# A two-layer graph network: layer 2's counts transposed by VectorE, the order of the passage between the layers given, and buffers of x split by use

## The chip, the cores and the metric

The kernel runs on one core of a Trainium2 chip. Times are microseconds of device time for one execution of the whole kernel. Engines are named as in the profile: PE (TensorE), PEld (its weight loads), DVE (VectorE), ACT (ScalarE), POOL (GpSimd, which issues the gathers), SP (which issues all other transfers).

## The reference

There are N = 2500 nodes of D = 1024 features and E = 80,000 edges, with `dst` sorted and skewed towards low nodes. Cut to what matters:

```python
# layer 1
support = relu(layernorm(x)) @ W0
x = x + segment_sum(support[src] * edge_weight[:, None], dst)
# layer 2: edge_index = [src, dst], with self loops
h = relu(layernorm(x)) @ W1.T + b
deg = counts of row (self loops included)
norm = deg[row] ** -0.5 * deg[col] ** -0.5
x = x + segment_sum(norm[:, None] * h[col], row)
```

`row` and `col` of layer 2 are src and dst with the self loops added. Layer 2 is thus out = x1 + S A S h, where A holds how often each pair of nodes is joined (plus the identity) and S is the diagonal of deg to the power -1/2.

## The kernel before

Rows are cut into NT = 20 tiles of P = 128 (the last has 68), features into KC = 8 slices of 128 or two halves of H = 512.

**Support.** For each row tile, layernorm, relu and 16 matmuls (L293) give the rows of `support`, which go to DRAM. This ends at about 470 us. Beside it, and in the stage that follows, VectorE and PE build the tables of counts: one-hot rows (L458, L460), a matmul (L462), and an addition into `counts` (L472), a 128 x 20 x 128 table for each destination tile, in three buffers that are taken in turn. `cleared` (L429) sets a table to zero on ACT (L435) before its first use. A finished table is stored to DRAM as `cnat` (L523) in 256-byte pieces.

**Gather stage.** The first DENSE = 4 tiles have so many edges that they are multiplied as dense tables against all of `support` (L657), two tiles and one half of the columns at a time. The 16 others ("thin" tiles) are handled in 378 blocks of 128 edges: POOL gathers 128 rows of `support` into `msg` (L616, eight buffers), ACT scales them and rounds to `hi` (L622), DVE computes the remainder `lo` (L624), and four matmuls with a one-hot matrix sum them by row (L628). When a thin tile is summed, `finish` (L568) adds x to the sums (L581; x is loaded at L163 by `load_rows`), stores x1 (L583) and normalizes; its rows are transposed on PE (L562, copied by ACT at L563), multiplied by W1 (L597, `second_rows`), get the bias on DVE (L601), and are stored as `hid_d` (L604). Dense tiles store their halves of x1 (L668) and come back through L573. Before the change both kinds of `xt`, the thin tiles' and the dense tiles', are buffers of one ring of two in the pool `work`.

How these streams are interleaved is decided by a planner in the kernel's own Python (`takes`, `count`, `others`), which keeps an estimate of the time of PE, DVE and ACT. On each engine instructions run in their order of issue. `order_behind` adds an ordering between two instructions of one engine and no wait between engines.

**Passage.** After the last gather the loop over layer 2 begins while the last tile's transposes and products are still running. `split(k)` (L810) loads hidden tile k (L812, three buffers, on SP), scales it by `dis` on ACT (hi, L813) and forms the remainder on DVE (lo, L814). `dis` holds deg to the power -1/2 with row t x 128 + p in partition p, column t (L787 to L790). `counts_of(r)` (L819) loads the counts of row tile r transposed, by one DMA transpose (L822), and ACT casts them to f32r in two halves of ten k (L828; four buffers `bT`).

**Rows.** `multiply` (L854) accumulates hi and lo of all 20 k in PSUM (L858, 80 matmuls a row tile), and `row` (L831) adds x1 and stores `out` (L836, L838). Row tiles 0 and 1 run as a pair, k by k behind `split`; 2 to 19 follow alone. The last tile runs its two column halves one after the other in one PSUM tile and adds both after the end.

Of the kernel before, what the change touches and what calls it, by code (L numbers as in the profile page):

```python
# [42 lines left out]
KEPT = 3  # L43

EARLY = 9

ORDER = (3, 4, 5, 6, 2, 7, 8, 9, 1, 10, 11, 12, 13, 0, 14, 15, 16, 17, 18, 19)

# [2 lines left out]
def direct(  # L51
# [41 lines left out]
    def rows(t):  # L93
        return min(P, N - t * P)
# [1 line left out]
    keep = ctx.enter_context(tc.tile_pool(name="keep", bufs=1))  # L96
    dram = ctx.enter_context(tc.tile_pool(name="dram", bufs=1, space=bass.MemoryType.DRAM))
    support = dram.tile([N, D], F32, name="support")
    cnat = dram.tile([NT, NT, P, P], F16, name="cnat")
    x1_d = [dram.tile([P, D], F32, name=f"x1_d{t}") for t in range(NT)]  # L100
    hid_d = [dram.tile([P, D], F32, name=f"hid_d{t}") for t in range(NT)]

    ident = keep.tile([P, P], F32, name="ident")
    make_identity(nc, ident)
# [51 lines left out]
        nc.scalar.activation(hn, xt, AF.Relu, scale=rstd[:, 0:1], bias=mean[:, 1:2])  # L156
        return hn

    def load_rows(t, pool):
        xt = pool.tile([P, D], F32, name="xt")  # L160
        if rows(t) < P:
            nc.vector.memset(xt, 0.0)
        nc.sync.dma_start(xt[:rows(t), :], x[t * P:t * P + rows(t), :])  # L163
        return xt
# [257 lines left out]
    KW = NT * max(w for _, w in WINDOWS)  # L422
    bases = {}
    ahead = None
    to_store = []
    dense = {}
    counts = {}

    def cleared(t):  # L429


        if t in counts:
            return
        counts[t] = cpool.tile([P, NT, P], F16, name="counts", bufs=3)
        i = nc.scalar.copy(counts[t].rearrange("p t w -> p (t w)"), zero.to_broadcast([P, NT * P]))  # L435
        if len(counts) > 3:
            order_behind(i, last_count)
# [117 lines left out]
    gpool = first.enter_context(tc.tile_pool(name="gather", bufs=2, side="right", reuse_waits="tile"))  # L555


    def transposed(v, into):
        for k0 in range(0, KC, 4):
            pT = psum.tile([P, 4, P], F32, name="pT")  # L560
            for k in range(4):
                nc.tensor.transpose(pT[:, k, :], v[:, (k0 + k) * P:(k0 + k + 1) * P], ident)  # L562
            nc.scalar.copy(into[:, k0:k0 + 4, :], pT)  # L563
            yield 0.7, 0.0, 0.6

    PIECES = 8
# [1 line left out]
    def finish(t, sums=None):  # L568


        if sums is None:
            xt = work.tile([P, D], F32, name="xt")
            nc.sync.dma_start(xt, x1_d[t])  # L573
            sum_ = work.tile([P, 1], F32, name="sum_")
            nc.vector.tensor_add(sum_, halves[t][:, 0:1], halves[t][:, 1:2])
            for _ in range(3):
                yield 0.0, 0.0, 0.0
        else:
            xt = load_rows(t, work)
            sum_ = work.tile([P, 1], F32, name="sum_")  # L580
            nc.vector.scalar_tensor_tensor(xt, sums.rearrange("p h d -> p (h d)"), 1.0, xt,  # L581
                                           op0=ALU.mult, op1=ALU.add, accum_out=sum_)
            nc.sync.dma_start(x1_d[t], xt)  # L583
# [7 lines left out]
    def second_rows(t, vT):  # L591

        hid = work.tile([P, D], F32, name="hn")
        for h in range(2):
            mm = psum.tile([P, 4, P], F32, name="pT").rearrange("p a b -> p (a b)")
            for k in range(KC):
                on_pe(nc.tensor.matmul(mm, vT[:, k, :], w1_sb[k][:, h * H:(h + 1) * H],  # L597
                                       start=(k == 0), stop=(k == KC - 1)))
                if k % 2 and k < KC - 1:
                    yield 1.75, 0.0, 0.0  # L600
            nc.vector.tensor_add(hid[:, h * H:(h + 1) * H], mm, bias[:, h * H:(h + 1) * H])  # L601
            if h == 0:
                yield 1.75, 0.65, 0.0
        nc.sync.dma_start(hid_d[t], hid)  # L604
        yield 1.75, 0.65, 0.0

    drawn = []
    last_hi = None

    def gathered(t, sums):  # L610
        nonlocal last_hi
        n = TILE_BLOCKS[t]
        for j in range(n):
            k = K0[t] + j
# [5 lines left out]
            nc.vector.tensor_scalar(oh, iota, row_p[:, k:k + 1], None, op0=ALU.is_equal)  # L620
            hi = gpool.tile([P, D], F32R, name="hi")
            last_hi = nc.scalar.activation(hi, msg, AF.Copy, scale=wgt_p[:, k:k + 1])  # L622
            lo = gpool.tile([P, D], F32R, name="lo")
            nc.vector.scalar_tensor_tensor(lo, msg, wgt_p[:, k:k + 1], hi.bitcast(F32),  # L624
                                           op0=ALU.mult, op1=ALU.subtract)
            for v in (hi, lo):
                for h in range(2):
                    i = nc.tensor.matmul(  # L628
# [9 lines left out]
    def multiplied(ts):  # L638
# [5 lines left out]
        for h in range(2):  # L644
            sums = psum_m.tile([P, 2, H], F32, name="mm")
            cols = slice(h * H, (h + 1) * H)
            for k0 in range(0, NT, 2):
# [7 lines left out]
                for k in (k0, k0 + 1):  # L655
# [151 lines left out]
    for k in range(EARLY):  # L807
        parts_of(k, early)

    def split(k):  # L810
        hf = work.tile([P, D], F32, name="rows", bufs=3)
        order_behind(nc.sync.dma_start(hf, hid_d[k]), drawn[-1])  # L812
        order_behind(nc.scalar.activation(his[k], hf, AF.Copy, scale=dis[:, k:k + 1]), last_hi)  # L813
        nc.vector.scalar_tensor_tensor(los[k], hf, dis[:, k:k + 1], his[k].bitcast(F32),  # L814
                                       op0=ALU.mult, op1=ALU.subtract)

    HALF = NT // 2

    def counts_of(r):  # L819

        cT = work.tile([P, NT, P], F16, name="cT")
        i = nc.sync.dma_start_transpose(out=cT.rearrange("p t s -> p (t s)"),  # L822
                                        in_=cnat[r].rearrange("t p d -> (t p) d"))
        order_behind(i, drawn[-1])
        bTs = []
        for k in (0, HALF):
            bTs.append(work.tile([P, HALF, P], F32R, name="bT", bufs=4))
            order_behind(nc.scalar.copy(bTs[-1], cT[:, k:k + HALF, :]), last_hi)  # L828
        return bTs

    def row(r, mm, hs):  # L831
        xh = work.tile([P, D], F32, name="rows", bufs=3)
        nc.sync.dma_start(xh, x1_d[r])
        for h in hs:
            cols = slice(h[0] * H, (h[-1] + 1) * H)
            nc.vector.scalar_tensor_tensor(xh[:, cols], mm.rearrange("p h d -> p (h d)")[:, cols],  # L836
                                           dis[:, r:r + 1], xh[:, cols], op0=ALU.mult, op1=ALU.add)
            nc.sync.dma_start(out[r * P:r * P + rows(r), cols], xh[:rows(r), cols])  # L838

    def all_placed():  # L840

# [12 lines left out]
    def multiply(bTs, mms, k, hs):  # L854
        for v in (his[k], los[k]):
            for bT, mm in zip(bTs, mms):
                for h in hs:
                    nc.tensor.matmul(mm[:, h, :], bT[k // HALF][:rows(k), k % HALF, :],  # L858
                                     v[:rows(k), h * H:(h + 1) * H],
                                     start=(k == 0 and v is his[k]), stop=(k == NT - 1 and v is los[k]))  # L860


    for rs in [(0, 1)] + [(r,) for r in range(2, NT)]:
        bTs = [counts_of(r) for r in rs]
        mms = [psum.tile([P, 2, H], F32, name="mm2", bufs=3) for r in rs]
        hs = ((0,), (1,)) if rs == (NT - 1,) else ((0, 1),)
        for part in hs:
            for k in range(NT):
                if rs[0] == 0:
                    split(k)  # L870
                multiply(bTs, mms, k, part)
        for r, mm in zip(rs, mms):
            row(r, mm, hs)
        if rs[0] == 4:
            all_placed()


def kernel(tc, edges, xT, *args):
# [338 lines left out]
```

## Time and profile before

| What | us |
|---|---|
| median of 3 runs (1697.03 to 1700.88) | 1699.94 |
| profiled execution, its own time | 1699.42 |
| span of its trace | 1697.6 |
| mean granted PE clock | 0.989 |

The span is what the trace covers; the execution's own time has some 1.8 us around it. Part of the groups of the profile, with their busy time and the mean of one instruction, then the idle time just ahead of them on their engine and who ended most of it:

```profile
L622 ACT ACTIVATE hi<-msg,wgt_p 128x1024 fp32r<-128x1024 f32 x378 | 425.6, 1146 | 279.1 <-PE mm L628 218.0
L624 DVE SCALAR_TENSOR_TENSOR lo<-msg,wgt_p,hi 128x1024 fp32r<-128x1024 f32 x378 | 478.1, 1280 | 31.9 <-ACT hi L622 23.6
L597 PE MATMUL pT<-w,vT 128*128 128x512 f32 x640 | 305.4, 595 | 0.0
L828 ACT CAST bT<-cT 128x1280 fp32r<-128x1280 f16 x40 | 50.2, 1263 | 262.9 <-PE mm L858 255.7
```

In a line such as the second, `lo<-msg,wgt_p,hi` names the tile written and the tiles read, `128x1024` partitions by elements, and `x378` the number of instructions. Matmuls overlap, so their mean is longer than the distance between two of them (0.226 us in the rows, 0.43 for L597). In a timeline a line starts with its start time and its length in us, and the bracket at its end tells how long its engine had been idle and what released it.

### The profile page before, as it was taken

How to read it: one execution, taken by the hardware profiler on the slowest of the kernel's cores; microseconds unless marked ns; L12 is line 12 of the kernel's file. 1: busy time of each engine (PE TensorE's matmuls, PEld its weight loads, DVE VectorE, ACT ScalarE, POOL GpSimd, SP SyncE). 2: the span in 40 equal slices, each digit the busy share in tenths (PEclk: the TensorE clock that was granted, in tenths of full speed). 3: DMA queues.
4: the chain of work that ended last, by engine and by line, in shares of the span. 5: the costliest groups of instructions: out<-in, count | busy, mean ns of one | idle time of the engine just before them, and what ended most of it. 6: DMA issues, size and time to landing. Idle time of an engine off the chain costs nothing.

```text
span 1697.6 us, 21231 instructions
## 1 busy us (share of the span) xinstructions
PE 1637.2 (96%) x6506; PEld 1033.2 (61%) x6506; DVE 1182.1 (70%) x3044; ACT 926.3 (55%) x1536; POOL 528.0 (31%) x501
## 2 busy tenths in 40 slices
PE   6999999999979998999999999999998999999998
PEld 2465555554435555565656666666654788888886
DVE  5778888889869997999999999998886410000000
ACT  3299999991125655666656666666666311111110
POOL 3000000000037665656656666666660000000000
PEclk9999999999989999999999999999999999999999
DMA  7512221123289998889899998999899634333320
GB/s 256 190 63 66 79 66 54 52 71 87 70 299 322 362 306 308 310 305 317 289 336 350 321 329 313 355 319 327 300 304 251 214 109 109 93 81 108 93 65 33
DMA packets 213657, 351.57 MB, mean 207 GB/s; under 512 B 115358, under 2 KB 134824, under 8 KB 213534
## 3 DMA queue, kind: packets, MB, share of 16 engines
q0 software_dynamic: 60592, 219.74, 36.9%
q1 hardware_dynamic: 152942, 130.39, 25.0%
q8 instruction: 53, 0.87, 0.2%
q14 instruction: 70, 0.57, 0.1%
HBM read 282.41 MB, written 54.56 MB: 198 GB/s over the span
## 4 chain that ended last, share of the span: by engine, by line
PE 63%; DMA 3%; issue 2%; DVE 2%; ACT 1%; POOL 1%; SPq 1%; DVEq 0%; POOLq 0%; ACTq 0%
PE mm L858 21%; PE mm L628 18%; PE pT L597 15%; PE mm L657 5%; PE cb L462 2%; DMA msg<-support,src_p 2%; PE pT L562 1%; DVE lo L624 1%; DMA rows<-hid_d 1%; PE mm L293 1%; DMA xt<-in_x 1%; SPq L822 0%; POOL msg L616 0%; DMA x_d<-xt 0%; ACT hi L622 0%
## 5 line engine op out<-in xcount | busy, mean ns | idle before, releaser
L622 ACT ACTIVATE hi<-msg,wgt_p 128x1024 fp32r<-128x1024 f32 x378 | 425.6, 1146 | 279.1 <-PE mm L628 218.0
L616 POOL DMA_INDIRECT msg<-support,src_p x378 | 480.4, 1271 | 273.1 <-DVE lo L624 117.9
L624 DVE SCALAR_TENSOR_TENSOR lo<-msg,wgt_p,hi 128x1024 fp32r<-128x1024 f32 x378 | 478.1, 1280 | 31.9 <-ACT hi L622 23.6
L293 PE MATMUL mm<-w,hT 128*128 128x512 f32 x640 | 317.0, 608 | 2.4 <-ACT hT L185 2.4
L597 PE MATMUL pT<-w,vT 128*128 128x512 f32 x640 | 305.4, 595 | 0.0
L628 PE MATMUL mm<-hi,oh_r 128*128 128x512 f32 x756 | 294.4, 470 | 5.0 <-DVE xt L581 5.0
L628 PE MATMUL mm<-lo,oh_r 128*128 128x512 f32 x756 | 264.1, 430 | 3.0 <-DVE lo L624 2.7
L469 ACT ACTIVATE wl<-oh_low,wpart 128x128 bf16<-128x128 bf16 x891 | 261.8, 394 | 0.0
L858 PE MATMUL mm<-lo,bT 128*128 128x512 f32 (+1 forms) x800 | 247.1, 390 | 0.0
L858 PE MATMUL mm<-hi,bT 128*128 128x512 f32 (+1 forms) x800 | 247.0, 390 | 0.0
L836 DVE SCALAR_TENSOR_TENSOR rows<-mm,dis,rows 128x1024 f32<-128x1024 f32 (+1 forms) x21 | 25.7, 1233 | 311.6 <-PE mm L858 311.6
L460 DVE TENSOR_SCALAR oh_key<-iota,key 128x200 bf16<-128x200 f16 (+12 forms) x675 | 195.6, 292 | 4.4 <-PE cb L476 4.3
L828 ACT CAST bT<-cT 128x1280 fp32r<-128x1280 f16 x40 | 50.2, 1263 | 262.9 <-PE mm L858 255.7
L628 PEld LDWEIGHTS mm<-hi,oh_r 128*128 128x128 f32 x756 | 140.5, 190 | 81.1 <-issue 45.4
L628 PEld LDWEIGHTS mm<-lo,oh_r 128*128 128x128 f32 x756 | 138.9, 189 | 70.1 <-DVE lo L624 22.0
L597 PEld LDWEIGHTS pT<-w,vT 128*128 128x128 f32 x640 | 120.9, 190 | 83.6 <-issue 68.7
L858 PEld LDWEIGHTS mm<-lo,bT 128*128 128x128 f32 (+1 forms) x800 | 150.2, 188 | 32.0 <-issue 0.5
L458 DVE TENSOR_SCALAR oh_low<-iota,low 128x128 bf16<-128x128 f16 x675 | 167.5, 252 | 2.3 <-ACT wl L469 1.7
L858 PEld LDWEIGHTS mm<-hi,bT 128*128 128x128 f32 (+1 forms) x800 | 150.1, 188 | 31.3
L472 DVE TENSOR_TENSOR counts<-cb,counts 128x200 f32 (+13 forms) x296 | 138.8, 469 | 43.1 <-PE cb L462 35.7
L657 PE MATMUL mm<-msg,dense 128*128 128x512 f32 (+1 forms) x320 | 153.8, 598 | 0.0
L293 PEld LDWEIGHTS mm<-w,hT 128*128 128x128 f32 x640 | 109.2, 195 | 65.8 <-issue 60.1
(172 smaller groups left out, 1179.4 us busy)
## 6 DMA issues: line engine op xcount, KB each, us to landing
msg<-support POOLq DMA_DIRECT2D x36, 512.0 KB
xt<-in_x SPq DMA_DIRECT2D x34, 512.0 KB
cnat<-counts SPq DMA_DIRECT2D x20, 640.0 KB
hid_d<-hn SPq DMA_DIRECT2D x20, 512.0 KB
rows<-hid_d SPq DMA_DIRECT2D x20, 512.0 KB
rows<-x_d SPq DMA_DIRECT2D x20, 512.0 KB
hT<-in_xT SPq DMA_DIRECT2D x19, 512.0 KB
support<-row SPq DMA_DIRECT2D x19, 512.0 KB
```

Of the source, the lines that this page charges most:

```text
L293: on_pe(nc.tensor.matmul(mm[:, h, :], vT[:, k, :], ws[k][:, h * H:(h + 1) * H], start=(k == 0), stop=(k == KC - 1)))
L458: nc.vector.tensor_scalar(oh_low, iota16[:, :P], low[:, k:k + 1], None, op0=ALU.is_equal)
L460: nc.vector.tensor_scalar(oh_key[:, :NT * w], iota16[:, :NT * w], key[:, k:k + 1], None, op0=ALU.is_equal)
L469: nc.scalar.activation(wl[:, i, :], oh_low, AF.Copy, scale=wpart[:, i, k:k + 1])
L472: nc.vector.tensor_tensor(to, cb[:, :NT * w].rearrange("p (t w) -> p t w", w=w), to, op=ALU.add)
L597: on_pe(nc.tensor.matmul(mm, vT[:, k, :], w1_sb[k][:, h * H:(h + 1) * H], start=(k == 0), stop=(k == KC - 1)))
L616: drawn.append(nc.gpsimd.indirect_dma_start(out=msg, out_offset=None, in_=support, in_offset=bass.IndirectOffsetOnAxis(ap=src_p[:, k:k + 1 ...
L622: last_hi = nc.scalar.activation(hi, msg, AF.Copy, scale=wgt_p[:, k:k + 1])
L624: nc.vector.scalar_tensor_tensor(lo, msg, wgt_p[:, k:k + 1], hi.bitcast(F32), op0=ALU.mult, op1=ALU.subtract)
L628: i = nc.tensor.matmul(sums[:, h, :], oh, v[:, h * H:(h + 1) * H], start=(j == 0 and v is hi), stop=(j == n - 1 and v is lo))
L657: m = nc.tensor.matmul(sums[:, i, :], dense[t][:rows(k), k, :], msg[:rows(k), k - k0], start=(k == 0), stop=(k == NT - 1))
L858: nc.tensor.matmul(mm[:, h, :], bT[k // HALF][:rows(k), k % HALF, :], v[:rows(k), h * H:(h + 1) * H], start=(k == 0 and v is his[k]), stop ...
```

## The change

It has five parts.

1. **Counts of layer 2.** `cnat` is laid out as [tile, row, tile, column], so that one row's counts are contiguous. A row tile's counts are loaded as they lie by four transfers in runs of 1280 bytes (`cN`, one buffer), transposed on DVE in blocks of 32 x 32 (one StreamTranspose of 128 x 2560 f16 a row tile, `cT`, one buffer), and cast by ACT with a reordering of 32-element runs. The blocks stay in their group of 32 partitions, so step k of the product takes hidden rows 32k to 32k + 31 of each of four quarters of 640 rows. The hidden rows are stored in five DRAM tiles in which those rows can be loaded by one transfer; steps 18 and 19 have 100 and 96 rows. `dis` is stored to DRAM and loaded again in the new order of rows (`dis_k`).
2. **Order of the passage.** Loads of hidden rows for k of 3 and more are ordered behind the loads of row 1's counts and behind the last x1 store; their hi behind ACT's last copy of the second transposes; their lo behind the last bias addition. The StreamTransposes stand behind the last lo of the gather stage. Row 2's counts are loaded behind the hidden rows of k = 10.
3. **First rows' scaling.** The first four hi of the gather stage are ordered behind the latest clearing of a counts table.
4. **x buffers by use.** Thin tiles have one buffer `xt`, dense tiles one buffer `dense_xt`, in place of the shared ring of two.
5. **Last row tile.** x1 is loaded ahead, the two column halves have PSUM tiles of their own, and each half is added and stored after its own matmuls.

On PE only the first pair of rows changes: between the two groups of four transposes only hi of row 0 for k = 0 stays, and the rest of that step follows the 32 products of L597. On SP, 80 loads of counts and 5 transfers of dis take the place of 20 DMA transposes. POOL's order is unchanged.

The diff, cut to its core:

```diff
-    cnat = dram.tile([NT, NT, P, P], F16, name="cnat")
+    cnat = dram.tile([NT, P, NT, P], F16, name="cnat")
+    dis_d = dram.tile([NT, P], F32, name="dis_d")
-    hid_d = [dram.tile([P, D], F32, name=f"hid_d{t}") for t in range(NT)]
+    hid_d = [dram.tile([4, P, D], F32, name=f"hid_d{q}") for q in range(NT // 4)]
...
-        i = nc.scalar.copy(counts[t].rearrange("p t w -> p (t w)"), zero.to_broadcast([P, NT * P]))
+        last_clear = nc.scalar.copy(counts[t].rearrange("p t w -> p (t w)"), zero.to_broadcast([P, NT * P]))
...
-            i = nc.sync.dma_start(cnat[:, t].rearrange("k p d -> p k d"), counts[t])
+            i = nc.sync.dma_start(cnat[:, :, t, :].rearrange("k p d -> p k d"), counts[t])
...
-            xt = work.tile([P, D], F32, name="xt")
+            xt = work.tile([P, D], F32, name="dense_xt", bufs=1)
...
-            xt = load_rows(t, work)
+            xt = load_rows(t, work, bufs=1)
...
             last_hi = nc.scalar.activation(hi, msg, AF.Copy, scale=wgt_p[:, k:k + 1])
+            if len(drawn) <= 4:
+                order_behind(last_hi, last_clear)
...
-                        xt = work.tile([P, 2, H], F32, name="xt")
+                        xt = work.tile([P, 2, H], F32, name="dense_xt", bufs=1)
...
+    nc.sync.dma_start(dis_d.rearrange("t p -> p t"), dis)
+    dis_k = keep.tile([P, NT], F32, name="dis_k")
+    for u in range(4):
+        nc.sync.dma_start(dis_k[32 * u:32 * u + 32, :],
+                          dis_d.rearrange("t p -> (t p)")[u * NT * 32:(u + 1) * NT * 32]
+                          .rearrange("(k i) -> i k", i=32))
...
     def split(k):
         hf = work.tile([P, D], F32, name="rows", bufs=3)
-        order_behind(nc.sync.dma_start(hf, hid_d[k]), drawn[-1])
...
+        of = hid_d[32 * k // P][:, 32 * k % P:32 * k % P + 32, :]
...
+        for j in i:
+            order_behind(j, drawn[-1] if k < AT_ONCE else loaded_counts[1])
+            if k >= AT_ONCE:
+                order_behind(j, last_x1)
...
+        order_behind(hi, last_hi if k < AT_ONCE else last_copy)
...
+        if k >= AT_ONCE:
+            order_behind(lo, last_bias)
...
-        cT = work.tile([P, NT, P], F16, name="cT")
-        i = nc.sync.dma_start_transpose(out=cT.rearrange("p t s -> p (t s)"),
-                                        in_=cnat[r].rearrange("t p d -> (t p) d"))
-        order_behind(i, drawn[-1])
+        cN = work.tile([P, 4, QUARTER], F16, name="cN", bufs=1)
+        for u in range(4):
+            i = nc.sync.dma_start(
+                cN[32 * u:32 * u + 32],
+                cnat[r].rearrange("(q i) t d -> i q (t d)", q=4)[:, :, u * QUARTER:(u + 1) * QUARTER])
+            order_behind(i, loads[HALF] if r == 2 else drawn[-1])
+        loaded_counts.append(i)
+        cT = work.tile([P, 4, NT, 32], F16, name="cT", bufs=1)
+        i = nc.vector.transpose(cT.rearrange("p q k i -> p (q k i)"), cN.rearrange("p q x -> p (q x)"))
+        order_behind(i, last_lo)
...
-            order_behind(nc.scalar.copy(bTs[-1], cT[:, k:k + HALF, :]), last_hi)
+            order_behind(nc.scalar.copy(bTs[-1].rearrange("p k q i -> p q k i"), cT[:, :, k:k + HALF, :]), last_hi)
...
-    for rs in [(0, 1)] + [(r,) for r in range(2, NT)]:
+    for rs in [(0, 1)] + [(r,) for r in range(2, NT - 1)]:
...
+    bTs = [counts_of(NT - 1)]
+    xh = x1_of(NT - 1)
+    for h in range(2):
+        mm = psum.tile([P, 2, H], F32, name="mm2", bufs=3)
+        for k in range(NT):
+            multiply(bTs, [mm], k, (h,))
+        row_of(NT - 1, xh, slice(h * H, (h + 1) * H), mm[:, h, :])
```

AT_ONCE is 3, QUARTER is 640 and HALF is 10.

More of the change, by code (lines that the diff above doesn't have):

```diff
@@ L45 @@
 EARLY = 9
+AT_ONCE = 3
 ORDER = (3, 4, 5, 6, 2, 7, 8, 9, 1, 10, 11, 12, 13, 0, 14, 15, 16, 17, 18, 19)
@@ L157, in normed, with load_rows @@
         return hn
-    def load_rows(t, pool):
-        xt = pool.tile([P, D], F32, name="xt")
+    def load_rows(t, pool, **bufs):
+        xt = pool.tile([P, D], F32, name="xt", **bufs)
         if rows(t) < P:
@@ L424, in direct @@
     ahead = None
+    last_clear = None
     to_store = []
@@ L434, in cleared @@
         counts[t] = cpool.tile([P, NT, P], F16, name="counts", bufs=3)
-        i = nc.scalar.copy(counts[t].rearrange("p t w -> p (t w)"), zero.to_broadcast([P, NT * P]))
+        nonlocal last_clear
+        last_clear = nc.scalar.copy(counts[t].rearrange("p t w -> p (t w)"), zero.to_broadcast([P, NT * P]))
         if len(counts) > 3:
-            order_behind(i, last_count)
+            order_behind(last_clear, last_count)
         if t < DENSE:
@@ L555, in direct @@
     gpool = first.enter_context(tc.tile_pool(name="gather", bufs=2, side="right", reuse_waits="tile"))
+    last_copy = last_bias = last_x1 = None
     def transposed(v, into):
+        nonlocal last_copy
         for k0 in range(0, KC, 4):
@@ L562, in transposed @@
                 nc.tensor.transpose(pT[:, k, :], v[:, (k0 + k) * P:(k0 + k + 1) * P], ident)
-            nc.scalar.copy(into[:, k0:k0 + 4, :], pT)
+            last_copy = nc.scalar.copy(into[:, k0:k0 + 4, :], pT)
             yield 0.7, 0.0, 0.6
@@ L582, in finish @@
                                            op0=ALU.mult, op1=ALU.add, accum_out=sum_)
-            nc.sync.dma_start(x1_d[t], xt)
+            nonlocal last_x1
+            last_x1 = nc.sync.dma_start(x1_d[t], xt)
             yield 0.0, 1.25, 0.0
@@ L591, in second_rows @@
     def second_rows(t, vT):
+        nonlocal last_bias
         hid = work.tile([P, D], F32, name="hn")
@@ L600, in second_rows @@
                     yield 1.75, 0.0, 0.0
-            nc.vector.tensor_add(hid[:, h * H:(h + 1) * H], mm, bias[:, h * H:(h + 1) * H])
+            last_bias = nc.vector.tensor_add(hid[:, h * H:(h + 1) * H], mm, bias[:, h * H:(h + 1) * H])
             if h == 0:
                 yield 1.75, 0.65, 0.0
-        nc.sync.dma_start(hid_d[t], hid)
+        nc.sync.dma_start(hid_d[t % (NT // 4)][t // (NT // 4)], hid)
         yield 1.75, 0.65, 0.0
     drawn = []
-    last_hi = None
+    last_hi = last_lo = None
     def gathered(t, sums):
-        nonlocal last_hi
+        nonlocal last_hi, last_lo
         n = TILE_BLOCKS[t]
@@ L622, in gathered @@
             last_hi = nc.scalar.activation(hi, msg, AF.Copy, scale=wgt_p[:, k:k + 1])
+            if len(drawn) <= 4:
+                order_behind(last_hi, last_clear)
             lo = gpool.tile([P, D], F32R, name="lo")
-            nc.vector.scalar_tensor_tensor(lo, msg, wgt_p[:, k:k + 1], hi.bitcast(F32),
-                                           op0=ALU.mult, op1=ALU.subtract)
+            last_lo = nc.vector.scalar_tensor_tensor(lo, msg, wgt_p[:, k:k + 1], hi.bitcast(F32),
+                                                     op0=ALU.mult, op1=ALU.subtract)
             for v in (hi, lo):
@@ L808, in direct, with valid @@
         parts_of(k, early)
+    QUARTER = NT * P // 4
+    HALF = NT // 2
+    loads, loaded_counts = [], []
+    def valid(k):
+        return min(P, 96 + max(N - 3 * QUARTER - 32 * k, 0))
     def split(k):
         hf = work.tile([P, D], F32, name="rows", bufs=3)
[L812 to L815, printed above, removed]
@@ L817, in direct @@
-    HALF = NT // 2
-    def counts_of(r):
-        cT = work.tile([P, NT, P], F16, name="cT")
-        i = nc.sync.dma_start_transpose(out=cT.rearrange("p t s -> p (t s)"),
-                                        in_=cnat[r].rearrange("t p d -> (t p) d"))
-        order_behind(i, drawn[-1])
+        of = hid_d[32 * k // P][:, 32 * k % P:32 * k % P + 32, :]
+        m = valid(k)
+        if m == P:
+            i = [nc.sync.dma_start(hf, of)]
+        else:
+            i = [nc.sync.dma_start(hf[:96], of[:3])]
+            if m > 96:
+                i.append(nc.sync.dma_start(hf[96:m], of[3, :m - 96, :]))
@@ new lines, in split @@
+        for j in i:
+            order_behind(j, drawn[-1] if k < AT_ONCE else loaded_counts[1])
+            if k >= AT_ONCE:
+                order_behind(j, last_x1)
+        loads.append(i[-1])
+        hi = nc.scalar.activation(his[k][:m], hf[:m], AF.Copy, scale=dis_k[:m, k:k + 1])
+        order_behind(hi, last_hi if k < AT_ONCE else last_copy)
+        lo = nc.vector.scalar_tensor_tensor(los[k][:m], hf[:m], dis_k[:m, k:k + 1], his[k][:m].bitcast(F32),
+                                            op0=ALU.mult, op1=ALU.subtract)
@@ L825, in counts_of, with x1_of @@
         bTs = []
         for k in (0, HALF):
-            bTs.append(work.tile([P, HALF, P], F32R, name="bT", bufs=4))
-            order_behind(nc.scalar.copy(bTs[-1], cT[:, k:k + HALF, :]), last_hi)
+            bTs.append(work.tile([P, HALF, 4, 32], F32R, name="bT", bufs=4))
+            order_behind(nc.scalar.copy(bTs[-1].rearrange("p k q i -> p q k i"), cT[:, :, k:k + HALF, :]), last_hi)
         return bTs
-    def row(r, mm, hs):
+    def x1_of(r):
         xh = work.tile([P, D], F32, name="rows", bufs=3)
@@ L833, in row, with row_of @@
         nc.sync.dma_start(xh, x1_d[r])
[L834 to L838, printed above, removed]
+        return xh
+    def row_of(r, xh, cols, sums):
+        nc.vector.scalar_tensor_tensor(xh[:, cols], sums, dis[:, r:r + 1], xh[:, cols], op0=ALU.mult, op1=ALU.add)
+        nc.sync.dma_start(out[r * P:r * P + rows(r), cols], xh[:rows(r), cols])
@@ L857, in multiply @@
                 for h in hs:
-                    nc.tensor.matmul(mm[:, h, :], bT[k // HALF][:rows(k), k % HALF, :],
-                                     v[:rows(k), h * H:(h + 1) * H],
+                    nc.tensor.matmul(mm[:, h, :],
+                                     bT[k // HALF][:valid(k), k % HALF].rearrange("p q i -> p (q i)"),
+                                     v[:valid(k), h * H:(h + 1) * H],
                                      start=(k == 0 and v is his[k]), stop=(k == NT - 1 and v is los[k]))
-    for rs in [(0, 1)] + [(r,) for r in range(2, NT)]:
+    for rs in [(0, 1)] + [(r,) for r in range(2, NT - 1)]:
         bTs = [counts_of(r) for r in rs]
         mms = [psum.tile([P, 2, H], F32, name="mm2", bufs=3) for r in rs]
[L866 to L871, printed above, removed]
+        for k in range(NT):
+            if rs[0] == 0:
+                split(k)
+            multiply(bTs, mms, k, (0, 1))
         for r, mm in zip(rs, mms):
-            row(r, mm, hs)
+            row_of(r, x1_of(r), slice(0, D), mm.rearrange("p h d -> p (h d)"))
         if rs[0] == 4:
             all_placed()
+    bTs = [counts_of(NT - 1)]
+    xh = x1_of(NT - 1)
+    for h in range(2):
+        mm = psum.tile([P, 2, H], F32, name="mm2", bufs=3)
+        for k in range(NT):
+            multiply(bTs, [mm], k, (h,))
+        row_of(NT - 1, xh, slice(h * H, (h + 1) * H), mm[:, h, :])
 def kernel(tc, edges, xT, *args):
```

## The prediction

> **What bounds the kernel now.** I read the page's first two parts, the chain of waits, the list of TensorE (PE) gaps above 0.6 us, and for each of the three largest the timeline of the engine named as releaser.
>
> ```profile
> PE 1637.2 (96%) x6506; PEld 1033.2 (61%) x6506; DVE 1182.1 (70%) x3044; ACT 926.3 (55%) x1536; POOL 528.0 (31%) x501
> ...
> DMA  7512221123289998889899998999899634333320
> ```
>
> PE is busy 1637 of 1697.6 us, so a change that leaves its matmuls alone can win only from its 60 us of gaps and from the half-clock time after them. The DMA row is the second limit: 8 to 9 tenths in the gather stage, about 470 to 1300 us. Three gaps make 19.9 us:
>
> ```profile
> 494.15 0.48 PE L462 MATMUL cb<-oh_key,oh_low 128*128 128x360 bf16 x1 [8.46 <-DVE oh_key L460]
> ...
> 655.05 1.19 PE L628 MATMUL mm<-hi,oh_r 128*128 128x512 f32 x2 [5.02 <-DVE xt L581]
> ...
> 1310.84 1.12 PE L562 MATMUL pT<-ident,hn 128*128 128x128 f32 x4 [6.38 <-DVE hn L601]
> ```
>
> The bracket is the idle time and what ended it. Each gap has its cause one or two engines back:
>
> ```profile
> 488.12 1.15 ACT L622 ACTIVATE hi<-msg,wgt_p 128x1024 fp32r<-128x1024 f32 x1 [16.29 <-DMA msg<-support,src_p]
> 490.09 1.15 ACT L622 ACTIVATE hi<-msg,wgt_p 128x1024 fp32r<-128x1024 f32 x1 [0.82 <-DMA msg<-support,src_p]
> 491.14 2.31 ACT L435 CAST counts<-zero 128x2560 f16<-128x2560 f32 x1
> ...
> 643.88 0.38 SPq L163 DMA_DIRECT2D xt<-in_x  x1
> 653.67 1.23 DVE L581 SCALAR_TENSOR_TENSOR xt<-mm,xt 128x1024 f32<-128x1024 f32 x1 [8.97 <-DMA xt<-in_x]
> ...
> 1302.75 7.78 SPq L812 DMA_DIRECT2D rows<-hid_d  x4
> 1307.71 1.15 ACT L813 ACTIVATE hi<-rows,dis 128x1024 fp32r<-128x1024 f32 x1 [6.91 <-DMA rows<-hid_d]
> 1308.90 1.28 DVE L814 SCALAR_TENSOR_TENSOR lo<-rows,dis,hi 128x1024 fp32r<-128x1024 f32 x1 [7.91 <-ACT hi L813]
> ```
>
> ACT waits 16.29 us for the first gathers while a clearing that needs none stands behind them; a load of x is issued 10 us before its use; the fourth hidden row is asked for at 1302.75, and a bias addition that PE needs stands behind its lo.
>
> **First rows' scaling behind a clearing.** The clearing moves ahead of the two hi. It needs only the store of the buffer's former tile, done by about 460, so it can run at 472 when ACT falls idle. The 8.46 us gap goes, and with it half a clock: the granted clock was 0.50 from 490 to 498, and four L657 took 3.44 us against 1.72 warm, 1.7 lost. Ideal gain 9.5 us. But what is late next is the gathers: the first L628 ran at 499.87, and from 476 to 505 the DMA share is about 1.0 (1.01 from 490 to 498, 397 GB/s); later hi already wait for messages at 536 to 558 and 567. PE's idle time let gathers run ahead, and part of the gain is returned there. Bounds 2 and 9.5; I take **5**.
>
> **x buffers by use.** The load for the first thin tile's successor waited for the dense halves' stores at 637 in the shared ring. With its own buffer it waits only for the former thin tile's normalization (577.6 + 1.2) and goes out near 580, 70 us early. The gap of 5.02 goes, and the cold time: the clock was 0.53 from 655 to 660, where L628 pairs stood 0.85 apart instead of 0.46, five of them, 2 us. The other thin tiles keep 25 to 75 us between normalization and next use; the last has about 8 (normalization to 1284.5, use at 1292.4), and a load lands in 4 to 5. Dense halves and finishes stay tens of us apart. 7 ideal; for more pressure on the gathers I take **6** (5 to 8).
>
> **Passage and transposes.** Before, from the first transposes (1302.46) to row 2 (1362.08) is 59.6 us: 6.38 of gap, and 15.5 for the 32 products against 32 x 0.43 = 13.8, 1.7 by the cold clock. In the new order every lo from row 3 on stands behind the last bias addition, so the second transposes come about 1303.4 and the products end near 1317.8. Then 156 of the pair's matmuls at the 0.226 us seen between 1327 and 1362 (154 in 34.8) give 1353.1, and 8.9 us are won.
>
> The same order costs a new gap. The StreamTranspose of row 2 stands on DVE behind row 0's final addition, which waits for the pair's last matmuls; row 2's cast and PE wait for it. PE then waits 1.28 (addition) + transpose + 1.26 (half a cast, L828's mean) less 0.25 (row 0 ends two matmuls early) plus about 0.4 of handover. A StreamTranspose is not in the trace. The nearest row is the only DVE operation that reads 128x2560 in the same type:
>
> ```profile
> L787 DVE TENSOR_REDUCE deg<-total 128x20 f32<-128x2560 f16 x1 | 2.8, 2809 | 0.0
> ```
>
> The 128x1024 additions agree: 1.28 against 0.69 for 512 is 0.59 per 512 elements, or 3.05 for 2560. Half of it, if two-byte data went twice as fast, is the lower bound, 1.4. The Trainium skill ("VectorE: DVE Perf Modes", The three transpose paths) states 311 ns for 128x128 in two-byte data, thus an estimate of 20 x 0.311 = 6.2 us. By the row the gap is 5.5, by the page 8.9. I take the row, since the 311 ns of so small an instruction hold its fixed part, paid once here. The same section speaks against the change: it says to keep to the DMA's own transposer, and that a plain copy with transposing strides is 19 times slower. The trace shows what that path costs here, an SP queue held 6.86 and 12.74 us ahead of the rows' loads; and the new loads don't transpose, they move runs of 1280 bytes, so that rule would price 80 transfers that the diff doesn't make.
>
> PE also starts row 2 cold. "TensorE: Matmul & The Clock Gate" (Part 1) says that an idle window of about 3.4 us halves the clock and that 3.4 us of work restore it; the trace's gaps of 5.02, 6.38 and 8.46 were each followed by 0.50 to 0.66. Some 1.8 more. The rows' loads for k from 3 are issued only after the x1 store and the counts' loads, with three buffers: about 6 us for three, 2.0 per row against PE's 1.81, from a head start of some 5 us, so 0 to 2 late. Sum: 8.9 - 5.5 - 1.8 - 0.7 = **+0.9** (-4 to +4). In later rows transpose, cast and addition fill some 7 of each row's 18.2 us and lie two rows ahead: nothing.
>
> **Last tile.** The second half's addition no longer waits behind the first's and the x1 load is early:
>
> ```profile
> 1689.69 1.41 DVE L836 SCALAR_TENSOR_TENSOR rows<-mm,dis,rows 128x512 f32<-128x512 f32 x2 [16.94 <-PE mm L858]
> 1690.47 0.92 SPq L838 DMA_DIRECT2D out<-rows  x2
> ```
>
> One of two additions leaves the tail: **+0.7**. PE's matmul count is the same.
>
> **Small costs.** dis goes out and back as 5,120 packets of 4 bytes near 1133, when DMA is 0.92 to 1.00 busy. The hardware queue's mean is 0.25 x 16 x 1697.6 / 152,942 = 44 ns a packet: 14 us on all 16 engines, under eight gathers of lead; the counts' stores keep 256-byte pieces, now 5 KB apart. Not under 0; up to 5; I take **0.4**. In SP's queue 80 short loads stand for 20 transposes that held it 2.2 to 6.9 us each; in the rows that queue is mostly free, so nothing.
>
> Sum: 5 + 6 + 0.9 + 0.7 - 0.4 = 12.2. From the profiled execution's own 1699.42 (span 1697.6) that is 1687.2; it lies 0.5 under the median of the runs, so 1687.7 on their scale; I say **1687.5**.
>
> **Rivals.** First, *all of the stalls' time is kept*: gathers keep up, as they do for 800 us with PE over 99% busy. 9.5 + 7.5 + 0.9 + 0.7 = 18.6: 1681. Against it: hi waits at 536 to 571. Second, *DMA decides the gather stage*: after each former stall the lead is consumed and the clearing brings 2 and the x buffers 4; with the new gap at row 2 at -1.5 the sum is 5: 1695. For it: shares near 1.0 for hundreds of us; against it, PE hardly waits for messages after 571. Third, on the other side, *the 4-byte packets stall the gathers*, at 1133 where all queues share 16 engines. If each holds an engine like the software queue's mean packet (0.369 x 16 x 1697.6 / 60,592 = 165 ns), they take 53 us of all engines; with eight gathers of lead worth some 18 us of PE time, up to 30 is exposed, and the kernel is slower as soon as more than 12 + 3.4 is; with 18.5 exposed, 1706. Against it: a 4-byte packet is no 3.6 KB message, and the load of 625 such elements at the start landed within 3.1 us of its issue. Fourth, *the gaps change place only* (the clearing waits for its store after all, row 2's transpose costs 6.2 and more): within 3.4 us of 1699.9.
>
> **How the numbers follow.** Sum as forecast 0.54 (1683 to 1692); everything kept 0.16; DMA decides 0.17; slower 0.08; no change 0.05. A measurement here can't tell 0.2% (3.4 us) from none. Faster 0.87, same 0.05, slower 0.08. The range takes the bounds: all favourable, 9.5 + 8 + 4 + 0.7 = 22: 1678; unfavourable, 2 + 5 - 4 + 0.7 - 5 = -1.3: 1701, cut to 1698 where no more than 2 in 10 is outside.
>
> **What would show it.** Right: no gap over 2 us on PE at 485 to 500 and at 650; the clearing at about 472; L608's products ending near 1306 (12 us earlier by then), one gap of 5 to 6 us before row 2 with DVE's StreamTranspose of about 3 us behind it, and a clock near 0.5 after it; row steps of 18.2 us. Wrong: new waits of hi for messages between 500 and 700 that sum to more than 5 us (the second rival), gaps at 1125 to 1180 (the third), or no gap at row 2.

## The result and the profile after

The changed kernel takes 1760.91 us (median of 3, 1760.81 to 1762.75) against 1699.94: slower, ratio 1.0366, 95% interval 1.0343 to 1.039. Its profiled execution has a span of 1759.1 us, 61.5 more than before.

PE runs the same matmuls in both kernels, in nearly the same order, so the n-th matmul of one trace can be set against the n-th of the other. That shows where the time was won and lost (us, after minus before, from the starts of the matmuls, counted from 0):

| matmul no. | what it is near | start before | start after | difference |
|---|---|---|---|---|
| 2000 | end of the support stage | 444.06 | 443.28 | -0.8 |
| 2200 | behind the first stall | 517.73 | 514.19 | -3.5 |
| 3000 | behind the x stall | 757.36 | 749.51 | -7.9 |
| 4300 | ahead of the transfers of dis | 1134.41 | 1125.61 | -8.8 |
| 4400 | behind them | 1162.45 | 1166.28 | +3.8 |
| 4800 | last gathers | 1281.13 | 1285.29 | +4.2 |
| 5100 | in row 2 | 1370.26 | 1433.16 | +62.9 |
| 6505 | last | 1689.26 | 1752.58 | +63.3 |

Two steps up carry the whole loss: 12.6 us between 1126 and 1166, and 58.7 us between the last gathers and row 2. The two stalls of the gather stage that the change aimed at brought 2.8 and 4.3 us. The page's busy tenths in 40 slices, of PE and of the granted clock, beside the DMA row:

```profile
PE   6999999999989999999999999979978689999998
...
PEclk9999999999999999999999999989999779999999
DMA  8412212132499998898999989988852243332320
```

At the 31st to 33rd slice, 1319 to 1451 us, PE falls to 8, 6 and 8 tenths, at a lowered clock in the last two, while the DMA row is at 2, 2 and 4: nothing looks saturated, which points to transfers that are slow by themselves. PE's timeline in that stretch, gaps in brackets, and the page's row for all matmuls of this kind:

```profile
1346.22 1.21 PE L906 MATMUL mm<-hi,bT 128*128 128x512 f32 x4 [1.66 <-ACT hi L854]
...
1351.24 1.72 PE L906 MATMUL mm<-hi,bT 128*128 128x512 f32 x4 [2.51 <-ACT hi L854]
...
L906 PE MATMUL mm<-hi,bT 128*128 128x512 f32 (+2 forms) x800 | 257.7, 404 | 32.9 <-ACT hi L854 28.3
```

From 1346 on each step of the first pair begins with a wait for hi. The row puts these waits at 28.3 us in all; much of the rest of the loss is matmuls at a lowered clock, four of which start to end take up to 2.08 us in place of 1.07. ACT's timeline says what hi waits for:

```profile
1350.05 1.15 ACT L854 ACTIVATE hi<-rows,dis_k 128x1024 fp32r<-128x1024 f32 x1 [3.87 <-DMA rows<-hid_d]
1355.15 1.15 ACT L854 ACTIVATE hi<-rows,dis_k 128x1024 fp32r<-128x1024 f32 x1 [3.95 <-DMA rows<-hid_d]
1360.30 1.15 ACT L854 ACTIVATE hi<-rows,dis_k 128x1024 fp32r<-128x1024 f32 x1 [4.01 <-DMA rows<-hid_d]
```

A hidden row tile arrives every 5.1 us, in place of the 1.81 us that PE took for a step before (8 matmuls of 0.226). The page's chain that ended last has the same culprit:

```profile
PE 46%; DMA 6%; DVE 3%; ACT 1%; issue 1%; SPq 0%; DVEq 0%; ACTq 0%
PE mm L906 19%; PE mm L641 12%; PE pT L608 11%; DMA rows<-hid_d 5%; PE mm L670 2%; DVE lo L637 1%; PE pT L571 1%; PE cb L468 1%; DVE lo L856 1%; DMA xt<-in_x 1%; ACT hi L633 0%; ACT hi L854 0%; ACT hn L160 0%; DVE xt L590 0%; DMA rows<-x_d 0%
```

The loads of hidden rows were 1% of the chain before and are 5% now. The other loss, and the stalls that the change aimed at, in PE's timeline:

```profile
493.56 2.08 PE L670 MATMUL mm<-msg,dense 128*128 128x512 f32 x2 [4.95 <-DMA msg<-support]
...
652.26 0.73 PE L641 MATMUL mm<-hi,oh_r 128*128 128x512 f32 x2 [0.86 <-ACT hi L633]
...
1163.56 1.22 PE L641 MATMUL mm<-lo,oh_r 128*128 128x512 f32 x2 [9.38 <-DVE lo L637]
...
1316.86 1.12 PE L571 MATMUL pT<-ident,hn 128*128 128x128 f32 x4 [10.11 <-ACT hn L160]
...
1423.19 1.22 PE L906 MATMUL mm<-hi,bT 128*128 128x512 f32 x2 [4.62 <-ACT bT L876]
```

The 8.46 us at 494 have become 4.95, ended by a load of `support` for the dense product; the 5.02 at 655 are gone. The 9.38 at 1163 are new, and 10.11 at 1316 stand in place of 6.38. There the last tile's transposes wait for its normalization on ACT, which stands behind hi of steps 1 and 2; hi of step 1 had waited 5.02 us for its row load (at 1307.77): the slow loads again. And there is the forecast gap ahead of row 2.

### The profile page after: what moved, and what is told of

Same layout as the page of the kernel before. It is cut to its first block, busy times and chain, and to the rows that moved or that the text cites. A ratio compares the mean times of both kernels' runs of the same rounds, so it can differ in the third digit from the quotient of the medians.

```text
span 1759.1 us, 21348 instructions
## 1 busy us (share of the span) xinstructions
PE 1658.2 (94%) x6506; PEld 1042.9 (59%) x6506; DVE 1239.1 (70%) x3064; ACT 927.4 (53%) x1536; POOL 527.8 (30%) x501
## 4 chain that ended last, share of the span: by engine, by line
PE 46%; DMA 6%; DVE 3%; ACT 1%; issue 1%; SPq 0%; DVEq 0%; ACTq 0%
PE mm L906 19%; PE mm L641 12%; PE pT L608 11%; DMA rows<-hid_d 5%; PE mm L670 2%; DVE lo L637 1%; PE pT L571 1%; PE cb L468 1%; DVE lo L856 1%; DMA xt<-in_x 1%; ACT hi L633 0%; ACT hi L854 0%; ACT hn L160 0%; DVE xt L590 0%; DMA rows<-x_d 0%
## 5 line engine op out<-in xcount | busy, mean ns | idle before, releaser
L906 PE MATMUL mm<-hi,bT 128*128 128x512 f32 (+2 forms) x800 | 257.7, 404 | 32.9 <-ACT hi L854 28.3
L906 PE MATMUL mm<-lo,bT 128*128 128x512 f32 (+2 forms) x800 | 256.3, 403 | 0.6
L906 PEld LDWEIGHTS mm<-hi,bT 128*128 128x128 f32 (+2 forms) x800 | 153.1, 193 | 73.4 <-ACT hi L854 36.4
L906 PEld LDWEIGHTS mm<-lo,bT 128*128 128x128 f32 (+2 forms) x800 | 155.6, 195 | 37.3 <-DVE lo L856 3.9
```

The source lines that it names most:

```text
L906: nc.tensor.matmul(mm[:, h, :], bT[k // HALF][:valid(k), k % HALF].rearrange("p q i -> p (q i)"), v[:valid(k), h * H:(h + 1) * H], start=( ...
```

## Experiments

**Theory E**: the row load's access pattern makes it slow. Its source has 4 as outermost dimension (four quarters of 32 rows), and by this theory such a transfer is carried by 4 of the 16 DMA engines: 128 packets of 4096 bytes, 32 an engine, at the trace's median of 159 ns for packets of this size, are 5.1 us. **Rival P**: the scattered addresses, or the new order in SP's queue, make it slow. For the loss at 1163, **theory Q**: the load of x stands in SP's queue behind loads of dis_k that wait for the store of dis; **rival C**: the 4-byte packets crowd the engines. The first four kernels below ran once each, beside one run of the kernel before, 1697.55. 40 later runs of the kernel before spread from 1692.12 to 1705.56, so a difference of 10 us between two single runs needs the traces beside it.

**Four transfers of 32 rows for each load**, same addresses (label rows16):

```diff
-            i = [nc.sync.dma_start(hf, of)]
...
+        i = [nc.sync.dma_start(hf[32 * q:min(32 * q + 32, m)], of[q, :min(32, m - 32 * q), :])
+             for q in range(-(-m // 32))]
```

> The changed kernel with each hidden-row load issued as four transfers of 32 rows each instead of one whose outermost dimension is 4; same DRAM addresses, same order. Theory E (engines): a transfer whose outermost dimension is 4 uses 4 of the 16 DMA engines; 128 packets of 4096 bytes at 159 ns are then 5.1 us a row, as seen. With 32 rows outermost all 16 work, a row lands every 2 us or less, and the time from the last gathers' products to row 2 falls from about 116 to about 58 us: the kernel near 1703 (1698 to 1710), with the gap at 1163 still there. Theory P (pattern or order): the loads are slow because their rows lie in four places 640 rows apart, or because of what stands ahead of them in SP's queue: 1751 to 1765.

1724.09 us: 37 less than the changed kernel, so P's "no change" falls, but 21 more than E had said. That forecast left out that a row tile now takes four issues on SP, inside a ring of three buffers. SP's timeline of this kernel, the durations of these issues (min/median/max in ns), and DVE's timeline:

```profile
1324.67 39.96 SPq L843 DMA_DIRECT2D rows<-hid_d  x66
1365.75 1.95 SPq L877 DMA_DIRECT2D rows<-x_d  x2
1367.75 0.90 SPq L861 DMA_DIRECT2D cN<-cnat  x2
...
L843 SPq DMA_DIRECT2D rows<-hid_d x79: 302/419/1358, 1292.2 to 1364.2; - x79
...
1330.41 1.28 DVE L852 SCALAR_TENSOR_TENSOR lo<-rows,dis_k,hi 128x1024 fp32r<-128x1024 f32 x1 [4.97 <-ACT hi L850]
...
1337.37 1.28 DVE L852 SCALAR_TENSOR_TENSOR lo<-rows,dis_k,hi 128x1024 fp32r<-128x1024 f32 x1 [1.05 <-ACT hi L850]
```

Four issues take 1.8 us (0.46 from start to start), and before the first of each row tile SP waits for the lo that frees a buffer: the lo at 1330.41 ends at 1331.69, and the next load goes at 1331.72. A buffer's round of issues, landing, hi and lo takes 7 us (1330.41 to 1337.37), so three buffers give a row tile every 2.3 us, against PE's 1.81. Row 2's counts are issued behind these loads, only at 1367.75, so PE waits 13.87 us for row 2's cast. One bottleneck gave way to the next.

**Two transfers with outermost dimension 2** (label rows2):

```diff
-            i = [nc.sync.dma_start(hf, of)]
+            i = [nc.sync.dma_start(hf[64 * q:64 * q + 64], of[2 * q:2 * q + 2]) for q in range(2)]
```

> The changed kernel with each hidden-row load of steps 0 to 17 issued as two transfers of two groups of 32 rows (outermost dimension 2). Theory E, with the engines always the lowest ones: both transfers sit on the same 2 engines, 64 packets of 159 ns on each, 10.2 us a row; 17 rows behind the first three at 5.1 us more are 87 us: 1848 (1835 to 1870). Theory E with other engines for the second transfer: 5.1 us a row, 1761. Theory P: 1755 to 1765.

1849.37 us, within 2 of what E says if both transfers go to the same two engines. ACT's timeline, and the table of stretches (columns: length, busy time of each engine, granted clock, DMA share of 16 engines, GB/s) of this kernel:

```profile
1392.20 1.15 ACT L854 ACTIVATE hi<-rows,dis_k 128x1024 fp32r<-128x1024 f32 x1 [8.83 <-DMA rows<-hid_d]
1402.32 1.15 ACT L854 ACTIVATE hi<-rows,dis_k 128x1024 fp32r<-128x1024 f32 x1 [8.97 <-DMA rows<-hid_d]
```

```profile
1400.00:1420.00 20.00, 7.56 (x16) 4.99 (x16) 2.57 (x2) 2.29 (x2) 0.00 (x0) 0.50 0.13 53
```

and the same table of the changed kernel and of the kernel before, in the pair:

```profile
1365.00:1385.00 20.00, 11.06 (x31) 7.33 (x32) 5.14 (x4) 4.59 (x4) 0.00 (x0) 0.84 0.28 108
```

```profile
1328.00:1348.00 20.00, 20.00 (x90) 16.52 (x88) 10.81 (x10) 11.51 (x11) 0.00 (x0) 1.00 0.64 211
```

A row tile comes every 10.1 us, and the share is 0.13, two engines of 16 (0.125). The changed kernel stands at 0.28, four engines (0.25) and a little for the counts. Half the engines, half the GB/s: 53 against 108.

**The kernel before with outermost dimension 4** (label before_rows4), the test from the other side:

```diff
-    hid_d = [dram.tile([P, D], F32, name=f"hid_d{t}") for t in range(NT)]
+    hid_d = [dram.tile([4, 33, D], F32, name=f"hid_d{t}") for t in range(NT)]
...
-        nc.sync.dma_start(hid_d[t], hid)
+        for q in range(4):
+            nc.sync.dma_start(hid_d[t][q, :32, :], hid[32 * q:32 * q + 32, :])
...
-        order_behind(nc.sync.dma_start(hf, hid_d[k]), drawn[-1])
+        order_behind(nc.sync.dma_start(hf, hid_d[k][:, :32, :]), drawn[-1])
```

> The kernel before, with its hidden rows kept in DRAM tiles of 4 x 33 rows, so that each load has an outermost dimension of 4 (and the stores go out as four transfers of 32 rows); everything else as before. Theory E: 5.1 us a row, the passage as slow as in the changed kernel: 1750 (1740 to 1762). Theory P: the rows lie nearly together and the order is the old one: 1700 (1697 to 1704).

1751.17 us. With nothing of the change in it but the shape of these loads, and four stores of 32 rows to fill them, the kernel before loses 53.6 us. ACT's timeline of it has the changed kernel's step of 5.1:

```profile
1355.52 1.15 ACT L814 ACTIVATE hi<-rows,dis 128x1024 fp32r<-128x1024 f32 x1 [3.84 <-DMA rows<-hid_d]
1360.58 1.15 ACT L814 ACTIVATE hi<-rows,dis 128x1024 fp32r<-128x1024 f32 x1 [3.91 <-DMA rows<-hid_d]
```

P falls with it: the four groups of 32 rows lie one row apart here, and the order of the passage is the old one.

The kept traces show the engines more directly. They record when a transfer's semaphore counts up: 16 times when a row load lands in the kernel before. In this kernel a store of hidden rows issued at 1348.53, beside the row loads, counts 12 times by 1350.73 and the last 4 times from 1360.01 to 1360.78, among the row loads' own counts. In the kernel with two transfers such a store, issued at 1342.62, counts 14 times by 1349.98 and the last two at 1361.49 and 1362.01. So four parts of 16, or two, are held by the row loads, and the same ones for all loads in flight: that is why three buffers don't help.

The Trainium skill has the rule ("DMA: Bandwidth & Descriptors", Why a DMA increments its semaphore by 16 and not by 1): the number of engines is the largest one up to 16 that divides the slowest (outermost) dimension of both patterns, source and destination. The steps of 5.1 and 10.1 us agree with it at 4 and at 2.

**dis_k's loads behind the load of x** (label dis_after_x):

```diff
-        nc.sync.dma_start(xt[:rows(t), :], x[t * P:t * P + rows(t), :])
+        x_loads[t] = nc.sync.dma_start(xt[:rows(t), :], x[t * P:t * P + rows(t), :])
...
-        nc.sync.dma_start(dis_k[32 * u:32 * u + 32, :],
+        order_behind(nc.sync.dma_start(dis_k[32 * u:32 * u + 32, :],
...
+                                       .rearrange("(k i) -> i k", i=32)), x_loads[15])
```

> The changed kernel with the four loads of dis_k ordered behind the load of x for tile 15 in SP's queue instead of ahead of it; the store of dis and its packets stay. Theory Q (queue): the 9.38 us gap near 1163 is the x load standing in SP's queue behind loads that wait for the store's landing; the gap and the cold time behind it go: 11 to 13 us less, 1749. Theory C (crowding): the 4-byte packets hold the DMA engines, and gathers or the x load stay late: not under 1757.

1750.71 us, 10.2 less, a little under the 11 to 13 forecast, and no PE gap above 0.6 us between 1070 and 1230: Q holds. SP's timeline of the changed kernel, then DVE's, shows the chain:

```profile
1123.67 0.37 SPq L804 DMA_DIRECT2D dis_d<-dis  x1
1139.40 11.53 SPq L807 DMA_DIRECT2D dis_k<-dis_d  x4
1151.05 3.95 SPq L167 DMA_DIRECT2D xt<-in_x  x1
...
1160.35 1.23 DVE L590 SCALAR_TENSOR_TENSOR xt<-mm,xt 128x1024 f32<-128x1024 f32 x1 [9.87 <-DMA xt<-in_x]
```

dis is sent at 1123.67; the loads that read it back can go only when it has landed, at 1139.40, and they hold SP for 11.53; tile 15's x goes at 1151.05, lands just ahead of 1160.35, and DVE, behind whose addition the lo stand, idles 9.87 us for it. C is not empty. That load of x took 9.2 us to land, beside the last packets of dis_k, and with the loads of dis_k behind it, it still took some 11 (issued at 1135.02, beside the packets of dis), but was early enough; and matmul 4400 still stands 1.5 us later against before than matmul 4300 does. The table of stretches of the changed kernel shows what the packets do to the engines:

```profile
1120.00:1130.00 10.00, 9.59 (x38) 5.95 (x37) 7.13 (x12) 6.87 (x8) 7.82 (x5) 1.00 1.03 205
1130.00:1135.00 5.00, 5.00 (x17) 2.92 (x16) 4.45 (x8) 4.97 (x7) 2.91 (x3) 1.00 1.04 63
```

At a share of 1.04 the engines move 63 GB/s, but PE is busy for all of those 5.00 us on gathers made earlier.

**Both mended** (label stored): hidden rows reordered when stored, four transfers a tile, so that each load is one contiguous transfer with 128 rows outermost; dis_k made on DVE.

```diff
-        nc.sync.dma_start(hid_d[t % (NT // 4)][t // (NT // 4)], hid)
+        q = t // (NT // 4)
+        for b in range(4):
+            nc.sync.dma_start(hid_d[t % (NT // 4) * 4 + b][32 * q:32 * q + 32, :], hid[32 * b:32 * b + 32, :])
...
+    for q in range(4):
+        for b in range(4):
+            nc.vector.tensor_copy(dis_k[32 * q:32 * q + 32, :].rearrange("p (a b) -> p a b", b=4)[:, :, b],
+                                  dis[32 * b:32 * b + 32, NT // 4 * q:NT // 4 * (q + 1)])
...
+        i = [nc.sync.dma_start(hf[:m], hid_d[k][:m, :])]
```

> The changed kernel with two parts of it mended: hidden rows are reordered when they are stored (four transfers of 32 rows a tile) and kept as 20 contiguous tiles, so that each load is one transfer with 128 rows outermost; and dis_k is made by 16 copies of 32 x 5 on DVE instead of through DRAM. If the engine count of the loads and the queue behind dis account for the whole loss, what is left is the forecast's gains as the changed kernel's trace shows them ahead of the passage (some 8 us), a passage about as long as before with its gap of 4.6 us at row 2, and 1.8 us at the end: 1690 (1686 to 1695). If the transposes or the order of the passage cost something of their own that the slow loads hid: 1698 or more.

1691.49 us, ratio to the kernel before 0.9954 (0.9938 to 0.9969). The two mended parts hold the whole loss: 69 us between this kernel and the changed one. PE's lead over before grows from 11.3 us at matmul 4850 to 19.1 at 4900, in the last products, and is 9.9 at 5200. So the new order wins 7.8 us, and the pair and row 2 give 9.2 back: from 1328 on hi waited for row loads up to 2.27 us, and PE waited for row 2's cast:

```profile
1350.48 1.22 PE L900 MATMUL mm<-hi,bT 128*128 128x512 f32 x2 [2.90 <-ACT bT L870]
```

The new order holds back the loads and lo of this stretch; that it is the cause of the pair's loss was not tried by itself.

**Row 2's transpose put ahead of row 0's addition** (label stored_t2):

```diff
+        if rs[0] == 0:
+            early_bTs = [counts_of(2)]
         for r, mm in zip(rs, mms):
```

> As the kernel with both parts mended, and the StreamTranspose of row 2 ahead of row 0's final addition on DVE. If the 4.62 us gap at row 2 is DVE's order alone, it and the half clock after it go: 5 to 7 us less than that kernel, 1684. If row 2's counts or buffers come no earlier, the same time.

1689.35 us, 0.994 (0.9919 to 0.9961): not told apart from the mended kernel. The premise was wrong there. In the mended kernel the transpose already stood ahead of that addition on DVE; both kernels show the same 2.90 us gap, with the transpose behind the last lo. In the changed kernel itself, where the transpose does stand behind the addition, this edit wasn't tried.

**Parts 3 and 4 alone on the kernel before** (labels before_p3, before_p4), their lines as in the diff of the change.

> The kernel before with the third part alone (the first four hi behind the clearing). If the gathers are late next, 2 to 3 us less: 1697. If the whole stall is kept as a gain, 9 us less: 1691.

> The kernel before with the fourth part alone (x buffers by use). The gap of 5 us at 655 and part of the cold time go: 4.5 to 6 us less, 1695; if gathers are late next, under 2 us less.

0.998 (0.997 to 0.9991), 3.4 us less, and 0.9977 (0.9964 to 0.9989), 3.9 less, each with the interval clear of 1. Part 3's interval, 1.5 to 5.1 us, leaves out the 9 of the whole stall; part 4's, 1.9 to 6.1, holds the 4.5 to 6 expected. With part 3 alone the 8.46 gap becomes

```profile
490.94 2.07 PE L661 MATMUL mm<-msg,dense 128*128 128x512 f32 x2 [3.06 <-DMA msg<-support]
```

a wait for a dense load: transfers are late next. The forecast had feared the gathers.

**Parts 3, 4 and 5 without 1 and 2** (label before_p345), beside the mended kernel run again (label stored_again):

> The kernel before with parts 3, 4 and 5 (clearing, x buffers, last tile) and without parts 1 and 2: the counts still come by DMA transposes and the passage keeps its old order. If parts 1 and 2, once mended, bring something of their own, this stays behind the mended kernel by the 6 us and more of the passage: 1694 or above. If they bring nothing net, it equals it: 1687 to 1692.

> The mended kernel once more, beside the kernel with parts 3 to 5 alone, on the same chip: 1688 to 1692.

1691.18 us, 0.9955 (0.9938 to 0.9972), and 1690.73, 0.9954 (0.9937 to 0.9972). They are not told apart, with intervals some 6 us wide, so DVE's transposes and the new order together show no net gain even when mended; the two were not tried apart. Both kernels beat the kernels before and after; the one with parts 3 to 5 is the simpler.

## Why the prediction was wrong, point by point

**The step that failed** is the passage's "about 6 us for three, 2.0 per row against PE's 1.81, from a head start of some 5 us, so 0 to 2 late". It took a row load to be what it was in the kernel before, where 128 rows lie outermost, and gave no reason; the diff's own `[:, ...:... + 32, :]` on a tile [4, 128, 1024] changes the shape. The term measured 5.1 us a row, since the loads share four DMA engines, and the stretch from matmul 4800 to 5100 was 58.7 us longer instead of 0.9 shorter. None of the rivals had it; the slower one sat elsewhere. What else that sum held was sound: the 8.9 us for the new order measured 7.8 in the mended kernel, where the loads are fast again.

**dis out and back**: 0.4 taken, 0 to 5 as bounds, 12.6 measured. The forecast priced the packets on the engines and let eight gathers of lead hide them, and so far it was right: PE stayed busy from 1130 to 1135. It did not ask what stands behind a load that waits on SP for a store to land. The third rival had the place and the sign, with another mechanism and 18.5 exposed where 12.6 was.

**First rows' scaling**: 5 taken (2 to 9.5), 2.8 in the changed kernel and 3.4 alone. The clearing ran at 470.95, as forecast, and transfers were late next; the one that PE waited for was a dense load and not a gather. Within its bounds, at the low end. The ideal gain was added up wrongly, 8.46 and 1.7 being 10.2 and not 9.5; nothing hung on it. The second rival's sign did not come: hi waited 14.4 us for messages between 500 and 700 against 11.0 before, 3.4 more and not over 5.

**x buffers**: 6 taken (5 to 8), 4.3 in the changed kernel and 3.9 alone; the load went out at 578.87 and the gap of 5.02 went, as forecast, but PE then waited for hi (0.86 and 0.79 us at 652 and 657). By matmuls 2200 and 3000 the same stretch brought 2.6 to 6.3 us in the single traces of the other kernels with both parts, so the shortfall is within their spread.

**Row 2's gap**: 5.5 forecast, 4.62 measured, released by the cast as said, with the clock at 0.50 from 1423 to 1426. The transpose was rightly taken from DVE's row, 2.8 us, and not from the skill's 311 ns, which made it 6.2. DVE's timeline of the changed kernel has it behind row 0's addition, and the list of groups from 1310 us on gives its mean:

```profile
1417.76 1.28 DVE L885 SCALAR_TENSOR_TENSOR rows<-mm,dis,rows 128x1024 f32<-128x1024 f32 x1 [1.71 <-PE mm L906]
1418.96 2.83 DVE L871 STREAM_TRANSPOSE cT<-cN 128x2560 f16<-128x2560 f16 x1
...
L871 DVE STREAM_TRANSPOSE cT<-cN 128x2560 f16<-128x2560 f16 x19 | 54.0, 2844 | 23.5 <-DMA cN<-cnat 22.7
```

**The end**: 0.7 forecast, 1.8 measured (63.3 at the last matmul, 61.5 in the span). **Rows**: nothing forecast, 0.4 measured.

The sum ahead of the passage without dis, 8.8 us less, against 11 forecast, was of the right size, though 0.8 of it lay ahead of the first stall and belongs to no part. The error is in two transfers: one priced without its shape, the other without what stands behind it in the queue.

## What to carry to other kernels

When a change alters a transfer's access pattern, price it anew: take the outermost dimension, divide the packets by the engines it allows, and multiply by the trace's time for a packet. A low DMA share beside a wait for a DMA can be the sign of too few engines. Here a reordering was cheaper at the store, where nobody waited, than at the load. A small round trip through DRAM can cost what stands behind its second half in the issuing queue, so look there first.

## What the runs showed of the hardware that was not expected

Loads of 512 KB with 4096-byte packets landed 5.1 us apart with 4 outermost and 10.1 apart as two transfers with 2, at a median of 159 ns a packet. Transfers in flight together did not share out over more engines: with 2 outermost the DMA share stayed at 0.13, and a store issued among them had 14 of its 16 counts 7.4 us after its issue and the last two only after 19.4. Sending 128 x 20 single numbers took from 1123.67 to about 1139 while gathers ran, and reading them back held the issuing queue for 11.53 us; 16 copies of 32 x 5 on DVE did the same in 16 x 0.21 = 3.4 us.
